# Attention over a long context: the division by the softmax sums goes from TensorE and VectorE to GpSimd by way of DRAM, and side work is dealt out evenly

## The chip, the cores and the metric

The kernel runs on one core of a Trainium2 chip. The metric is device time in microseconds of one launch. The core has five instruction streams: TensorE (PE, matrix products, with its weight loads shown as PEld), VectorE (DVE), ScalarE (ACT), GpSimd (POOL) and SyncE (SP), which here issues nearly all DMAs. Each stream runs its instructions in order and waits for the others by semaphores. SBUF is the on-chip memory with 128 partitions; PSUM is where PE writes and where DVE and ACT read its results.

## The reference

Four layers of cross-attention are applied to x (2048 tokens of 256) over one context of 1601 rows of 512. Layers L0, L2 and L3 are of one kind, "masked": 16 heads of 64.

```python
q = hidden_states @ Wq;  k = encoder_hidden_states @ Wk;  v = encoder_hidden_states @ Wv
logits = jnp.einsum('bhqd,bhkd->bhqk', q, k) * scale
logits = logits + col_bias[None, None, :, :]
probs = jax.nn.softmax(logits, axis=-1)
out = jnp.einsum('bhqk,bhkd->bhqd', probs, v)
out = out @ Wo + bo + residual
```

`col_bias` is zero but in up to four columns of the context, which the token indices name; there it is -20 for suppressed query rows. Layer L1 is "grouped": x is normalised by its root mean square, there are 16 query heads of 16 that share 4 key and value heads, and no bias. Everything is float32.

## The kernel before

**Tiles and units.** The tokens are four blocks b of 512 queries (QB), the context 13 chunks of 128 keys (NT = 13, the last has 65). Heads are taken in pairs: a "block" of a masked layer is one pair with its own slices of Wq, Wk, Wv and Wo (8 blocks a layer), a block of L1 has two pairs ("subs"; 4 blocks). A "unit" is one pair and one b. There are 128 units: 32 of each layer, 96 of them masked.

**Steps.** One loop of `N + NT + DELAY + LAG` steps, with N = 128*13, deals out the work, a chunk c a step. In a step the unit ka makes scores for its chunk ca; the unit kb, 15 steps behind, subtracts the row maxima and takes exponentials of its chunk cb; the unit kv, one step more behind, multiplies chunk cv with the values. In steps ca = 0 and 1 the maxima of the unit just scored are found and spread (L805, L806, L818). PE, DVE and ACT keep this written order: the last lines of the kernel add it as a dependency. POOL and SP get their order from the framework's scheduler.

**A masked step.** PE makes scores of both heads into a tile of `ps_s` (L751; two buffers, one tile is 128x1024). ACT copies it to a tile `p` of SBUF (L763; 17 buffers), DVE keeps a running maximum `top` (L768), and later adds the negated maxima (L834). ACT takes the exponential in place (L841). POOL adds the chunk to `sums` (L844 for chunks 0 and 1 together, L846 after that). PE multiplies with the values into `po` (L869). The trace has two matmul records for each float32 matmul of 512 columns.

**The tail of a unit.** After its last chunk ACT copies `po` to `oT` (L875, one buffer, 128 rows = 2 heads of 64, 512 queries). Four more pieces follow: `denominators` transposes `sums` with eight PE transposes into a tile of `ps_s` (L888), DVE reduces it (L889) and takes reciprocals (L890) into `rden`, 128x8, and POOL copies them 64 times side by side into `by` (L899). `divide` transposes `by` with four PE transposes (L907) and multiplies with `oT` on DVE (L911). `project(k)`, k = 0 and 1, is one matmul with Wo (L917), which DVE adds to the residual `xs` (L923). In L1 the sums are an extra row of the values' product; they come by four small matmuls (L894) and a reciprocal (L897).

**Pieces.** What isn't a chunk of a unit is a "piece", popped between the chunks at the end of a step: the tail of the unit before, the next unit's queries (L420, two pieces), and the next block's keys (L369, in groups of four pieces, one for the 65 keys) and values (L384, in groups of two). A group that has begun is finished before another queue is looked at. `urgent` (tail, queries) goes before `fill` (keys, values). Each step earns credit, and each piece costs one. No piece is popped in the two steps of a masked unit's maxima. Nearly every piece writes a tile of `ps_m` ("pm"), which has one buffer.

```python
def step(self, share):
    self.credit = min(self.credit + share, 2.0)
    while self.credit >= 1.0:
        self.pop()
        self.credit -= 1.0
...
pieces.step(max(1.0, (pieces.left() + 6 * after_this) / steps))
```

**Loads.** The transposed context lies in DRAM (`ctxT`); slices of it (`ct`, three buffers) come in by SP just ahead of the pieces that use them (L204), as do x (L735), the weights (L345, two buffers each) and Wo (L353).

Of the kernel before, what the change touches and what calls it, by code (L numbers as in the profile page):

```python
# [10 lines left out]
FP = mybir.dt.float32  # L11
# [18 lines left out]
def tile_cross_attention_stack(ctx: ExitStack, tc: tile.TileContext, t: dict, out: bass.AP):  # L30
# [167 lines left out]
    def context_slice(a, n):  # L198

        step = NCT if n <= 256 else NCT // 2  # L200
        tiles = []
        for k in range(0, NCT, step):
            ct = work.tile([P, step, 2 * QB // step], FP, name="ct", bufs=3)
            nc.sync.dma_start(out=ct[:, :, :n], in_=ctxT_dram[:, k : k + step, a : a + n])  # L204
            tiles.append(ct)
        return lambda k, b, m: tiles[k // step][:, k % step, b - a : b - a + m]
# [121 lines left out]
    class Masked:  # L328
# [8 lines left out]
        def load(self, n):  # L337
# [4 lines left out]
            u.wk = weights.tile([P, NCT, P], FP, name="wk")  # L342
            u.wv = weights.tile([P, NCT, P], FP, name="wv")
# [85 lines left out]
    class Grouped:  # L429
# [34 lines left out]
        def load(self, n):  # L464
# [3 lines left out]
            if n == 0:  # L468
# [14 lines left out]
                self.wk = weights.tile([P, NCT, 2, 64], FP, name="wk")  # L483
                self.wv = weights.tile([P, NCT, 64], FP, name="wv")
# [180 lines left out]
    def keep(l, b):  # L665
        nc.sync.dma_start(out=xT_dram[l][b], in_=xs[:, b])

    def normalize(l, b):
# [3 lines left out]
        def squares():  # L672
            held["x"] = work.tile([P, NC, QB], FP, name="xT")
            nc.scalar.activation(held["x"], xs[:, b], AF.Square)

# [10 lines left out]
        def divide(q):  # L686
# [8 lines left out]
            if q == QT - 1:  # L695
                nc.sync.dma_start(out=xT_dram[l][b], in_=held["x"])

        return [[squares], [rms], *([lambda q=q: divide(q)] for q in range(QT))]

    def rows_out(b):  # L700
# [9 lines left out]
        for q0 in (0, half):  # L710
# [5 lines left out]
            )  # L716


    class Unit:
# [116 lines left out]
        def exp(self, c, spare):  # L836
            u = self.u
            a, m = TCH[c]
            if self.masked:
                p = self.p[c]  # L840
                nc.scalar.activation(p[:m], p[:m], AF.Exp)  # L841
                if c == 1:
                    self.sums = work.tile([P, 2, QB], FP, name="sums")
                    nc.gpsimd.tensor_tensor(self.sums, self.p[0], p, ALU.add)  # L844
                elif c:
# [35 lines left out]
        def denominators(self):  # L881

            rden = self.rden = small.tile([P, 2, QT], FP, name="rden")
            if self.masked:
                pt = ps_s.tile([P, 2, QT, P], FP, name="s")
                for h in range(2):
                    for q in range(QT):
                        nc.tensor.transpose(pt[:, h, q, :], self.sums[:, h, ts(q, P)], ident)  # L888
                nc.vector.tensor_reduce(rden, pt, AX.X, ALU.add)  # L889
                nc.vector.reciprocal(rden, rden)  # L890
            else:
# [6 lines left out]
            self.by = work.tile([P, QT, 2, 64], FP, name="by", bufs=1)  # L898
            nc.gpsimd.tensor_copy(  # L899
                self.by,  # L900
                rden.rearrange("p h (q o) -> p q h o", o=1).to_broadcast((P, QT, 2, 64)),
            )

        def divide(self):
            pr = ps_m.tile([P, QB], FP, name="pm")
            for q in range(QT):
# [258 lines left out]
```

## Time and profile before

| | |
|---|---|
| median of 3 runs | 5645.32 us (5644.31 to 5645.62) |
| the profiled execution | 5653.54 us, its span 5651.8 us |
| PE busy | 5321.4 us, 94% |
| DVE, ACT, POOL busy | 71%, 57%, 50% |
| mean granted TensorE clock | 0.98 |
| DMA | 252.88 MB, mean 45 GB/s |

A group's line gives source line, engine, operation, output and inputs with partitions x elements and type, the count, busy time in us and mean ns of one instruction; behind the last bar stands the idle time of the engine just before these instructions and what ended it. Busy time of a group counts overlapping records once. A line of the waits gives who waited for whom, the total in us, how often and the longest. In the order of time a line begins with start and duration; a remark in brackets is the idle time of that engine just before, and who ended it.

### The profile page before, as it was taken

The numbers are of one execution on the slowest core, as the hardware profiler recorded it, in microseconds if no ns is written. First come the engines' busy times: TensorE is split into PE (matmuls) and PEld (weight loads), VectorE is DVE, ScalarE is ACT, GpSimd is POOL, SyncE is SP. The second block draws the span as 40 slices with busy tenths as digits, with TensorE's granted clock in tenths as the row PEclk, the third lists the DMA queues.
The fourth block names the chain that finished last, engine by engine and source line by source line (L and its number), as shares of the span: only waits on it lengthen the run. The fifth ranks groups of instructions, "written<-read, shape, count | busy, mean of one in ns | idle before, by whom it ended". The sixth has DMA issues, their size and how long they took to land.

```text
span 5651.8 us, 59516 instructions
## 1 busy us (share of the span) xinstructions
PE 5321.4 (94%) x22444; PEld 1865.2 (33%) x22444; DVE 4013.6 (71%) x4140; ACT 3196.2 (57%) x3513; POOL 2837.7 (50%) x1380
## 2 busy tenths in 40 slices
PE   6999999998889999999999999999999999999997
PEld 3333333332323333233233333333333333333332
DVE  3777777777765555555567777777777777777786
ACT  2666666665433434333456666666666666666665
POOL 1766666665410000000056666666666666666676
PEclk8999999999889999999999999999999999999998
DMA  4112211111100000001012111212111121111100
GB/s 135 32 57 60 59 49 53 55 56 44 39 20 5 9 9 9 9 13 52 15 51 61 56 54 49 57 56 59 46 56 55 54 59 49 53 56 52 54 17 15
DMA packets 209744, 252.88 MB, mean 45 GB/s; under 512 B 43529, under 2 KB 155401, under 8 KB 209456
## 3 DMA queue, kind: packets, MB, share of 16 engines
q1 hardware_dynamic: 206192, 243.69, 14.8%
q8 instruction: 177, 2.90, 0.2%
q0 software_dynamic: 1152, 3.28, 0.2%
q10 hardware_dynamic: 2112, 2.10, 0.1%
q14 instruction: 111, 0.91, 0.1%
HBM read 235.27 MB, written 13.76 MB: 44 GB/s over the span
## 4 chain that ended last, share of the span: by engine, by line
PE 78%; ACT 7%; POOL 7%; DVE 5%; issue 2%; DMA 0%; SPq 0%; ACTq 0%; POOLq 0%; DVEq 0%
PE po L869 24%; PE s L751 20%; PE pm L384 6%; PE pm L369 5%; PE pm L917 5%; POOL sums L844 4%; ACT p L763 4%; ACT p L841 3%; POOL sums L846 3%; PE s L850 2%; PE s L784 2%; PE pm L420 2%; PE s L805 2%; PE b L818 2%; PE s L855 2%
## 5 line engine op out<-in xcount | busy, mean ns | idle before, releaser
L846 POOL TENSOR_TENSOR sums<-sums,p 128x1024 f32<-128x1024 f32 (+1 forms) x1056 | 2499.2, 2367 | 1097.9 <-ACT p L841 1084.8
L763 ACT COPY p<-s 128x1024 f32<-128x1024 f32 (+1 forms) x1248 | 1263.4, 1012 | 1434.0 <-PE s L751 1138.3
L869 PE MATMUL po<-p,v 128*64 128x512 f32 (+1 forms) x6656 | 1821.7, 626 | 36.5 <-ACT p L841 34.7
L768 DVE TENSOR_TENSOR top<-s,top 128x1024 f32<-128x1024 f32 (+1 forms) x1056 | 1291.5, 1223 | 753.9 <-ACT p L763 749.4
L751 PE MATMUL s<-q,kT 64*128 64x512 f32 (+1 forms) x4992 | 1426.3, 648 | 117.6 <-DVE top L768 116.4
L834 DVE TENSOR_TENSOR p<-p,b 128x1024 f32<-128x1024 f32 (+1 forms) x1248 | 1504.7, 1206 | 2.4 <-PE b L818 2.0
L841 ACT ACTIVATE p<-p 128x1024 f32<-128x1024 f32 (+1 forms) x1248 | 1321.5, 1059 | 110.3 <-DVE p L834 109.4
L869 PEld LDWEIGHTS po<-p,v 128*64 128x64 f32 (+1 forms) x6656 | 332.0, 136 | 1032.1 <-issue 698.9
L899 POOL COPY by<-rden 128x512 f32<-128x512 f32 x128 | 78.5, 613 | 1111.8 <-DVE rden L897 1083.9
L751 PEld LDWEIGHTS s<-q,kT 64*128 64x128 f32 (+1 forms) x4992 | 370.7, 182 | 732.7 <-issue 454.6
L859 ACT ACTIVATE p<-s 128x1024 f32<-128x1024 f32 (+1 forms) x283 | 289.8, 1024 | 451.0 <-PE s L855 450.9
L844 POOL TENSOR_TENSOR sums<-p 128x1024 f32<-128x1024 f32 x96 | 226.5, 2360 | 434.2 <-ACT p L841 434.2
L789 DVE TENSOR_REDUCE row_top<-s 128x2 f32<-128x1024 f32 x261 | 318.6, 1221 | 122.9 <-PE s L784 121.9
L384 PEld LDWEIGHTS pm<-wv,ct 128*128 128x128 f32 (+1 forms) x2392 | 284.7, 187 | 218.9 <-issue 215.9
L384 PE MATMUL pm<-wv,ct 128*128 128x128 f32 (+1 forms) x2392 | 337.6, 286 | 0.5 <-ACT v L389 0.5
L369 PE MATMUL pm<-ct,wk 128*128 128x512 f32 (+1 forms) x736 | 315.8, 544 | 2.7 <-ACT kT L374 2.7
L917 PE MATMUL pm<-o,wo 128*128 128x512 f32 x512 | 292.0, 653 | 7.1 <-DVE xs L923 2.9
L859 ACT ACTIVATE p<-b 128x1024 f32<-128x1024 f32 (+1 forms) x133 | 136.2, 1024 | 217.8 <-PE b L855 217.8
L923 DVE TENSOR_TENSOR xs<-pm,xs 128x512 f32<-128x512 f32 x232 | 158.4, 683 | 90.4 <-PE pm L917 90.4
L806 DVE TENSOR_REDUCE ntop<-s 128x8 f32<-128x1024 f32 x96 | 117.6, 1225 | 130.9 <-PE s L805 130.6
L789 DVE TENSOR_REDUCE row_top<-b 128x2 f32<-128x1024 f32 x123 | 150.2, 1221 | 62.2 <-PE b L784 61.6
L420 PE MATMUL pm<-xT,wq 128*128 128x512 f32 x336 | 188.5, 644 | 0.0
(191 smaller groups left out, 3279.2 us busy)
## 6 DMA issues: line engine op xcount, KB each, us to landing
ct<-ctxT SPq DMA_DIRECT2D x288, 512.0 KB, 3.8
xT<-xT SPq DMA_DIRECT2D x104, 512.0 KB, 3.5
ct<-ctxT SPq DMA_DIRECT2D x48, 130.0 KB, 2.6
wk<-in_L_xattn_Wk_dram SPq DMA_DIRECT2D x24, 256.0 KB, 4.4
wv<-in_L_xattn_Wv_dram SPq DMA_DIRECT2D x24, 256.0 KB, 3.1
xT<-xs SPq DMA_DIRECT2D x12, 512.0 KB, 2.6
wq<-in_L_xattn_Wq_dram SPq DMA_DIRECT2D x24, 128.0 KB, 2.1
wo<-in_L_xattn_Wo_dram SPq DMA_DIRECT2D x24, 128.0 KB, 2.1
```

Source lines behind the costliest of these rows:

```text
L369: nc.tensor.matmul(u.pk[:, :n], u.wk[:, k, :], ct(k, a, n), start=(k == 0), stop=(k == NCT - 1),)
L384: nc.tensor.matmul(u.pv[:m, c - c0, :], ct(k, a, m), u.wv[:, k, :], start=(k == 0), stop=(k == NCT - 1),)
L751: nc.tensor.matmul(s[:m, h, :], self.u.kT[r, a : a + m], self.q[r, :], start=True, stop=(a != TAIL),)
L763: nc.scalar.copy(p[:m], s[:m])
L768: nc.vector.tensor_tensor(self.top[:m], s[:m], self.top[:m], ALU.max)
L789: nc.vector.tensor_reduce(self.top[:, :, q, k : k + 1], s, AX.X, ALU.max)
L834: nc.vector.tensor_tensor(self.p[c][:m], self.p[c][:m], self.less[:m], ALU.add)
L841: nc.scalar.activation(p[:m], p[:m], AF.Exp)
L844: nc.gpsimd.tensor_tensor(self.sums, self.p[0], p, ALU.add)
L846: nc.gpsimd.tensor_tensor(self.sums[:m], self.sums[:m], p[:m], ALU.add)
L869: nc.tensor.matmul(self.po[r, :], u.v[:m, c, r], self.p[c][:m, h, :], start=(c == 0), stop=(c == NT - 1),)
L917: nc.tensor.matmul(py, wo[:, ts(k, P)], self.o, start=True, stop=True)
```

## The change

The first chunk of `sums` is copied by POOL at c = 0, and every later chunk is added; before, the first addition took chunks 0 and 1 together. The denominators come a head at a time, four transposes each, into `ps_m` in place of `ps_s`, and cost half a credit each. `rden` is written to DRAM by SP (`cols`) and read back twice with a step of zero across 64 partitions, so that `by` holds a head's 512 reciprocals on each of that head's 64 rows. `divide` is one multiplication on POOL, in place in `oT`, for no credit; the four transposes of `by`, POOL's copy and DVE's multiplication are gone. `project` reads `oT`.

The tail is no longer put on the queue at once: queries are due one step after they were, the denominators three steps after the unit's last chunk, `divide` and `project` eight steps after it. A step earns what is left divided by the steps left, no longer at least one, and a piece tells its cost. Context tiles are loaded as their forerunners are used up, three ahead. `wk` and `wv` have one buffer each. The loop runs ten steps longer.

```diff
@@ -197,13 +197,16 @@
         step = NCT if n <= 256 else NCT // 2
-        tiles = []
-        for k in range(0, NCT, step):
-            ct = work.tile([P, step, 2 * QB // step], FP, name="ct", bufs=3)
+        tiles = {}
+        def load(k):
+            tiles[k] = ct = work.tile([P, step, 2 * QB // step], FP, name="ct", bufs=3)
             nc.sync.dma_start(out=ct[:, :, :n], in_=ctxT_dram[:, k : k + step, a : a + n])
-            tiles.append(ct)
-        return lambda k, b, m: tiles[k // step][:, k % step, b - a : b - a + m]
+        loads = [lambda k=k: load(k) for k in range(0, NCT, step)]
+        return lambda k, b, m: tiles[k - k % step][:, k % step, b - a : b - a + m], loads
...
@@ -339,8 +342,8 @@
             u.wq = weights.tile([P, NC, P], FP, name="wq")
-            u.wk = weights.tile([P, NCT, P], FP, name="wk")
-            u.wv = weights.tile([P, NCT, P], FP, name="wv")
+            u.wk = weights.tile([P, NCT, P], FP, name="wk", bufs=1)
+            u.wv = weights.tile([P, NCT, P], FP, name="wv", bufs=1)
             for to, w in ((u.wq, "Wq"), (u.wk, "Wk"), (u.wv, "Wv")):
...
@@ -480,8 +483,8 @@
                         nc.gpsimd.tensor_copy(self.last_k[:, g, to], ident[:, j : j + 16])
-                self.wk = weights.tile([P, NCT, 2, 64], FP, name="wk")
-                self.wv = weights.tile([P, NCT, 64], FP, name="wv")
+                self.wk = weights.tile([P, NCT, 2, 64], FP, name="wk", bufs=1)
+                self.wv = weights.tile([P, NCT, 64], FP, name="wv", bufs=1)
                 for half in range(2):
...
@@ -714,6 +720,16 @@
+    def on_all_partitions(cols, to):
+        rows = dram.tile([2, P, QT], FP, name="cols", bufs=4)
+        with nc.allow_non_contiguous_dma(reason="1024 values, four at a time"):
+            nc.sync.dma_start(out=rows.rearrange("h p q -> p h q"), in_=cols)
+        for tile_, heads_ in to:
+            src = rows[heads_].rearrange("(o h) p q -> o (h p q)", o=1)
+            nc.sync.dma_start(out=tile_, in_=src.to_broadcast(tile_.shape))
...
@@ -839,10 +855,10 @@
                 nc.scalar.activation(p[:m], p[:m], AF.Exp)
-                if c == 1:
+                if c == 0:
                     self.sums = work.tile([P, 2, QB], FP, name="sums")
-                    nc.gpsimd.tensor_tensor(self.sums, self.p[0], p, ALU.add)
-                elif c:
+                    nc.gpsimd.tensor_copy(self.sums, p)
+                else:
                     nc.gpsimd.tensor_tensor(self.sums[:m], self.sums[:m], p[:m], ALU.add)
...
@@ -878,15 +894,18 @@
-        def denominators(self):
-            rden = self.rden = small.tile([P, 2, QT], FP, name="rden")
+        def denominators(self, h):
+            if h == 0:
+                self.rden = small.tile([P, 2, QT], FP, name="rden")
+            rden = self.rden
             if self.masked:
-                pt = ps_s.tile([P, 2, QT, P], FP, name="s")
-                for h in range(2):
-                    for q in range(QT):
-                        nc.tensor.transpose(pt[:, h, q, :], self.sums[:, h, ts(q, P)], ident)
-                nc.vector.tensor_reduce(rden, pt, AX.X, ALU.add)
+                pt = ps_m.tile([P, QT, P], FP, name="pm")
+                for q in range(QT):
+                    nc.tensor.transpose(pt[:, q, :], self.sums[:, h, ts(q, P)], ident)
+                nc.vector.tensor_reduce(rden[:, h, :], pt, AX.X, ALU.add)
+                if h == 0:
+                    return 0.5
                 nc.vector.reciprocal(rden, rden)
...
@@ -895,26 +914,27 @@
                 nc.vector.reciprocal(rden, pd.rearrange("p q h -> p h q"))
-            self.by = work.tile([P, QT, 2, 64], FP, name="by", bufs=1)
-            nc.gpsimd.tensor_copy(
-                self.by,
-                rden.rearrange("p h (q o) -> p q h o", o=1).to_broadcast((P, QT, 2, 64)),
+            by = work.tile([P, P, QT], FP, name="by", bufs=1)
+            on_all_partitions(
+                rden,
+                [(by[self.rows(h)].rearrange("r p q -> r (p q)"), slice(h, h + 1)) for h in range(2)],
             )
+            self.by = by.rearrange("r p q -> r q p")
+            return 0.5 if self.masked else 1.0
+        def denominator_groups(self):
+            return [[lambda h=h: self.denominators(h)] for h in range(2 if self.masked else 1)]
         def divide(self):
-            pr = ps_m.tile([P, QB], FP, name="pm")
-            for q in range(QT):
-                nc.tensor.transpose(
-                    pr[:, ts(q, P)], self.by[:, q].rearrange("p h o -> p (h o)"), ident
-                )
-            self.o = work.tile([P, QB], FP, name="o", bufs=1)
-            nc.vector.tensor_tensor(self.o, pr, self.oT, ALU.mult)
+            oT = self.oT.rearrange("r (q p) -> r q p", p=P)
+            nc.gpsimd.tensor_tensor(oT, oT, self.by, ALU.mult)
+            return 0.0
             wo = self.layer.wo(self.u, self.sub)
-            nc.tensor.matmul(py, wo[:, ts(k, P)], self.o, start=True, stop=True)
+            nc.tensor.matmul(py, wo[:, ts(k, P)], self.oT, start=True, stop=True)
             to = xs[:, self.b, k, :]
...
@@ -923,9 +943,7 @@
         def finish_groups(self):
-            return [[self.denominators], [self.divide]] + [
-                [lambda k=k: self.project(k)] for k in range(NC)
-            ]
+            return [[self.divide]] + [[lambda k=k: self.project(k)] for k in range(NC)]
...
@@ -976,19 +994,20 @@
                 if not queue:
-                    return
+                    return 1.0
                 self.now.extend(queue.popleft())
-            self.now.popleft()()
+            cost = self.now.popleft()()
+            return 1.0 if cost is None else cost
-            self.credit = min(self.credit + share, 2.0)
+            self.credit = min(self.credit, 0.9) + share
             while self.credit >= 1.0:
-                self.pop()
-                self.credit -= 1.0
+                self.credit -= self.pop()
...
@@ -1010,33 +1029,30 @@
         nxt = made[l, n] = layer.load(n)
-        slices = {}
-        ahead = deque()
-        def load(name):
-            if name in ahead:
-                ahead.remove(name)
-                kind, c, a, width = name
-                slices[kind, c] = context_slice(a, width)
+        slices, loads = {}, deque()
                 if name:
-                    ahead.append(name)
-                def head(name=name, piece=group[0]):
-                    load(name)
-                    if name and ahead:
-                        load(ahead[0])
-                    piece()
-                found.append([head, *group[1:]])
+                    kind, c, a, width = name
+                    slices[kind, c], tiles = context_slice(a, width)
+                    loads.extend(tiles)
+                    each = len(group) // len(tiles)
+                    def read(j, piece, each=each):
+                        piece()
+                        if (j + 1) % each == 0 and loads:
+                            loads.popleft()()
+                    group = [lambda j=j, piece=piece, r=read: r(j, piece) for j, piece in enumerate(group)]
+                found.append(list(group))
             return found
         first, second = map(with_loads, layer.key_groups(nxt, slices))
+        for _ in range(min(3, len(loads))):
+            loads.popleft()()
...
@@ -1062,9 +1078,10 @@
     N = len(units) * NT
+    due = {}
     turn = 0
-    for step in range(N + NT + DELAY + LAG):
+    for step in range(N + NT + DELAY + LAG + 10):
         ka, ca = divmod(step, NT)
...
@@ -1077,6 +1094,7 @@
                 start_block(i)
+        top = of[ka - 1] if 0 < ka <= len(units) and ca < 2 else None
         three = not (scoring and scoring.masked) and not (exping and exping.masked)
...
@@ -1086,7 +1104,6 @@
-        top = of[ka - 1] if ka and ca < 2 and ka - 1 < len(units) else None
         if step == 3:
...
@@ -1104,10 +1121,11 @@
             ahead = unit_of(ka + 1)
-            pieces.urgent.extend(ahead.layer.unit_groups(ahead))
+            due.setdefault(step + 1, []).extend(ahead.layer.unit_groups(ahead))
         if valuing and cv == NT - 1:
-            pieces.urgent.extend(valuing.finish_groups())
-            pieces.urgent.extend(after(kv))
+            due.setdefault(step + 3, []).extend(valuing.denominator_groups())
+            due.setdefault(step + 8, []).extend(valuing.finish_groups() + after(kv))
+        pieces.urgent.extend(due.pop(step, ()))
...
@@ -1116,7 +1134,7 @@
             steps = NT - ca + (NT - 2) * after_this
-            pieces.step(max(1.0, (pieces.left() + 6 * after_this) / steps))
+            pieces.step((pieces.left() + 5 * after_this) / steps)
         elif not scoring:
     pieces.flush(pieces.urgent)
```

Three functions that issue no matmul (`keep`, `squares`, the normalising `divide`) now return a cost of 0.0; these lines are left out.

More of the change, by code (lines that the diff above doesn't have):

```diff
@@ L674, in squares @@
             nc.scalar.activation(held["x"], xs[:, b], AF.Square)
+            return 0.0
         def rms():
@@ L696, in divide @@
                 nc.sync.dma_start(out=xT_dram[l][b], in_=held["x"])
+            return 0.0
         return [[squares], [rms], *([lambda q=q: divide(q)] for q in range(QT))]
@@ L897, in denominators @@
                 nc.vector.reciprocal(rden, pd.rearrange("p q h -> p h q"))
-            self.by = work.tile([P, QT, 2, 64], FP, name="by", bufs=1)
-            nc.gpsimd.tensor_copy(
-                self.by,
-                rden.rearrange("p h (q o) -> p q h o", o=1).to_broadcast((P, QT, 2, 64)),
-            )
+            by = work.tile([P, P, QT], FP, name="by", bufs=1)
+            on_all_partitions(
+                rden,
+                [(by[self.rows(h)].rearrange("r p q -> r (p q)"), slice(h, h + 1)) for h in range(2)],
+            )
+            self.by = by.rearrange("r p q -> r q p")
+            return 0.5 if self.masked else 1.0
+        def denominator_groups(self):
+            return [[lambda h=h: self.denominators(h)] for h in range(2 if self.masked else 1)]
         def divide(self):
-            pr = ps_m.tile([P, QB], FP, name="pm")
-            for q in range(QT):
-                nc.tensor.transpose(
-                    pr[:, ts(q, P)], self.by[:, q].rearrange("p h o -> p (h o)"), ident
-                )
-            self.o = work.tile([P, QB], FP, name="o", bufs=1)
-            nc.vector.tensor_tensor(self.o, pr, self.oT, ALU.mult)
+            oT = self.oT.rearrange("r (q p) -> r q p", p=P)
+            nc.gpsimd.tensor_tensor(oT, oT, self.by, ALU.mult)
+            return 0.0
         def project(self, k):
```

## The prediction

> **What bounds the kernel now.** Four views, in this order: busy time by engine, TensorE's waits, the groups of instructions by shape, and the order of time around one wait.
>
> ```profile
> span 5651.8 us, 59516 instructions
> PE 5321.4 (94%) x22444; PEld 1865.2 (33%) x22444; DVE 4013.6 (71%) x4140; ACT 3196.2 (57%) x3513; POOL 2837.7 (50%) x1380
> ```
> ```profile
> PE s L751 <- DVE top L768: 116.4, 71, 2.7
> PE pm L907 <- POOL by L899: 55.9, 79, 4.4
> ```
>
> PE is busy 94% of the span: every PE microsecond taken away or added moves the end. Its two largest waits belong to the tail of a unit, which the change rewrites.
>
> ```profile
> L917 PE MATMUL pm<-o,wo 128*128 128x512 f32 x512 | 292.0, 653 | 7.1 <-DVE xs L923 2.9 <-DVE xs L921 2.3 <-DVE o L911 1.9
> L907 PE MATMUL pm<-ident,by 128*128 128x128 f32 x512 | 90.5, 303 | 56.1 <-POOL by L899 55.9
> L846 POOL TENSOR_TENSOR sums<-sums,p 128x1024 f32<-128x1024 f32 x960 | 2271.8, 2366 | 1025.6 <-ACT p L841 1015.1 <-ACT ka L517 3.5 <-ACT v L389 2.4
> L899 POOL COPY by<-rden 128x512 f32<-128x512 f32 x128 | 78.5, 613 | 1111.8 <-DVE rden L897 1083.9 <-DVE rden L890 26.8
> L791 DVE TENSOR_REDUCE row_top<-b 128x8 f32<-128x520 f32 x11 | 7.7, 701 | 10.0 <-PE b L784 9.9
> ```
>
> An ordinary masked step, in order of time (start, duration):
>
> ```profile
> 3402.84 1.13 PE L751 MATMUL s<-q,kT 64*128 64x512 f32 x4
> 3404.91 1.12 PE L369 MATMUL pm<-ct,wk 128*128 128x512 f32 x2
> 3404.98 1.06 ACT L841 ACTIVATE p<-p 128x1024 f32<-128x1024 f32 x1
> 3405.11 1.22 DVE L768 TENSOR_TENSOR top<-s,top 128x1024 f32<-128x1024 f32 x1 [0.77 <-ACT p L763]
> 3405.96 1.13 PE L751 MATMUL s<-q,kT 64*128 64x512 f32 x4
> 3406.18 2.37 POOL L846 TENSOR_TENSOR sums<-sums,p 128x1024 f32<-128x1024 f32 x1 [0.76 <-ACT p L841]
> ```
>
> The step is 3.12 us. PE comes to its piece 2.07 us after the step's start; DVE finishes `top` at 3.49; POOL starts the step's sum at 3.34 and ends it at 5.71. These offsets carry the sum below. Now a tail whose two parts fall into one step:
>
> ```profile
> 4342.24 1.09 PE L888 MATMUL s<-ident,sums 128*128 128x128 f32 x8
> 4342.71 1.01 ACT L763 COPY p<-s 128x1024 f32<-128x1024 f32 x1 [1.84 <-POOL sums L844]
> 4344.90 1.21 DVE L889 TENSOR_REDUCE rden<-s 128x8 f32<-128x1024 f32 x1
> 4347.11 0.61 POOL L899 COPY by<-rden 128x512 f32<-128x512 f32 x1
> 4347.77 0.66 PE L907 MATMUL pm<-ident,by 128*128 128x128 f32 x4 [4.44 <-POOL by L899]
> 4348.36 1.97 PE L751 MATMUL s<-q,kT 64*128 64x512 f32 x4
> ```
> ```profile
> 4348.00:4352.00 4.00, 4.00 (x12) 0.88 (x10) 2.35 (x3) 1.58 (x2) 0.00 (x0) 0.57 0.00 0
> ```
>
> A wait of 4.44 us for a product of POOL, and after it the granted clock is 0.57 of full over 4 us (the column after the five engines): the scores take 1.97 us instead of 1.13, the values 1.89 instead of 1.08. The clock costs 1.7 us on top. After the like wait at 2890.8 us the four groups of matmuls that follow lose 2.8 us, at 0.50 for 6.5 us.
>
> **What goes.** (a) 512 transposes of `by`: 90.5 us of PE. (b) The waits before them: 56. (c) The masked denominators no longer take a tile of `ps_s`, so the next scores needn't wait for `top`: 112 of the 116.4 us (68 waits of 1.65 directly behind L888). The copy at c=0 frees p[0] a step earlier, which ends ACT's 1.84 us; PE feels that only through (c), so it is counted once. Sum 259. The copy itself (two 512s at 613 ns, 1.2 us a unit), the multiply and twelve sums make 31 us of POOL in a unit of some 43: covered by the steps' POOL idle (0.76 us and more before each sum). DVE loses L911 and has slack. The even sharing leaves 112 masked steps without a piece instead of 32; such a step takes 2.07 us of PE at 3 isolated places of the trace, so PE's work only changes place: nothing, or up to 15 us if DVE (2.43 us a step) falls behind.
>
> **What comes, counted in the built program of the changed kernel.**
>
> (1) A wait on `pm`, which has one buffer. Head 1's four transposes, or another piece, follow head 0's or head 1's denominators within one step 86 times (63 times head 1 behind head 0). The first four end 2.07+0.55 = 2.62 us into the step; the reduction comes behind `top` (3.49) and takes 0.70 (row of 520); PE goes on at 4.25. Each 1.65 us; two L917 in one step waited up to 1.4 in this trace with 0.55 us more work ahead, which makes it 1.3 to 1.95. Sum 142.
>
> (2) The projection waits for the multiply. The denominators are due five steps before `divide`, but a key group of four pieces is not interrupted, so they slip. Of four units of a block the last denominators come 3, 2, 1 and 1 steps before the projection. `divide` costs no credit, so `project(0)` follows in the same step; and on POOL the multiply stands behind the sum of that very step in 45 masked units. In these PE arrives at 2.07, the sum ends at 5.71, and a multiply of 1.2 us (half of L846) ends at 6.9, with its handover 7.0. Units whose previous step held the two heads' wait have DVE 0.9 us late against PE, which its `subtract` hands on: 5.5; the others 4.9. I take 5.2: 234 us. The chain that feeds it, reciprocal 0.2, a write to DRAM, two broadcasts and their issues, is bounded by DMA rows:
>
> ```profile
> wq<-in_L_xattn_Wq_dram SPq DMA_DIRECT2D x24, 128.0 KB, 2.1
> wo<-in_L_xattn_wo_dram SPq DMA_DIRECT2D x16, 16.0 KB, 1.7
> ```
>
> Write 1.7 to 2.1, reads 2.1 plus one issue of 0.35: about 4.5 us, so `by` lands some 10.3 us after the start of the denominators' step, and the sum (10.5 to 11 on that scale) is still last. In 19 units with two steps between, the multiply follows the previous step's sum and ends 0.4 us late: 10 with a few odd ones. With three steps it is hidden behind them. On SP a context load stands between write and broadcasts in 19 units and waits for PE's key piece; it is issued at about 5.4, its 512 KB take 3.8, and the broadcasts behind it still land before that sum ends. So xT and context loads, which are two tiles (some 12 us) ahead, stay hidden too; their cover ends if SP blocks longer than that. `wk`, `wv` with one buffer are loaded before their first use by half a block or more: nothing.
>
> (3) The clock. 45 waits above 4.44 us, each with 1.7 to 2.8 behind it as measured: 2.3, so 104 us. Nothing is the lower bound, since most of the 1.65 us waits had no drop; but three of three above 4.4 us had one.
>
> (4) Layer L1 (32 units). POOL is free there; the chain is reciprocal 0.57 after the products, DRAM and back 4.6, multiply 1.2 and handovers: 6.6 us. A step without a piece is 2.1 us. The projection comes in the same step in 6 units (6.6), one step later in 13 (4.5), two in 9 (2.4): 40+58+22 = 120; clock for the first 19: 44. Before, L1's tail had no wait.
>
> (5) The end: DRAM and back in place of two short steps: 5.
>
> Sum 142+234+10+104+120+44+5 = 659, less 259: +400. The profiled execution took 5653.54 (span 5651.8), 8 above the median of 5645.3; so 5645+400 = 6045.
>
> **Two rules of the Trainium skill against this.** *GPSIMD Engine Reference*, Performance pitfalls, says that POOL reading SBUF in steps above 8 bytes pays about half again; `by` is read in steps of 16 bytes, and no run here shows it. By that the multiply is an estimated 1.8 us and 73 waits (45+28) grow by 0.6, +44. *TensorE: Matmul & The Clock Gate*, Part 1, says that an idle window of 3.4 us halves the clock until a busy one; the row above agrees (0.57). By one such window, 1.7 us a wait, (3) and (4) would be 109 instead of 148.
>
> **Rivals.**
> *Faster: PE's arrival is late enough that the multiply is never waited for.* Place: `project(0)`. If the product stands ready, what remains is -259+142, 5530. It decides below 117 us of such waits in all, 1.6 us on each of 73. For it: half of the masked units have two or three steps of cover. Against: 45 multiplies stand behind a sum that ends 3.6 us after PE's arrival.
> *Waits, but the clock holds:* +400-148, 5895. For: 68 waits of 1.65 us passed mostly undisturbed. Against: three waits of 4.44 us, three drops.
> *SP becomes the bound:* broadcasts held behind loads that wait for PE, 3 us more on the 73 waits, +220, 6265. For: 19 units have a load between. Against: SP's loads land in 2 to 4 us.
> *The spread makes no difference* (within 0.2%): the two sums would have to cancel.
>
> **How the numbers follow.** Forecast 0.72, clock holds 0.12, SP 0.08, faster 0.06, same 0.02. 0.2% (11 us) is about what a measurement of this kernel can tell from no change. Low end of the forecast: (1) at 1.3 us is 112, (2) at 4.9 is 220, the clock at 1.0 behind the 45 is 45, L1 with a chain of 5.8 is 6x5.8+13x3.7+9x1.6 = 97, the end and the rest 10: 484-259 = +225, 5870. High end: 86x1.95 = 168; 45x6.5 = 292 (the broadcasts 1 us late behind a context load); 30 for the 19 units; the clock 64x3.3 = 211 (half of 6.5 us); L1 with 7.5, 45+70+30 = 145; 25 for steps without pieces and the end: 871-259 = +612, 6257. I give 5880 to 6250; it takes in the clock rival. Faster 0.06, same 0.02, slower 0.92.
>
> **What would show it.** Right: PE waits on POOL before the projection, 4.9 to 5.5 us some 45 times and 2 to 7 us some 28 times in L1; about 86 waits of 1.65 on DVE between denominators; no L907; a granted clock below 0.95 in masked slices. Wrong: a wait for POOL below 120 us in total, a multiply that starts ahead of the step's sum, or DMAs back in under 2 us together.

## The result, and the profile after

The changed kernel takes 6248.9 us (median of 4 runs, 6246.4 to 6255.0), the kernel before took 5644.8 beside it: a ratio of 1.107 [1.105, 1.109], 604 us slower (by the ratio 606 on the 5645.3 from which the forecast starts), where the forecast was +400 and its range ended at +605. The direction and the place of the waits were as forecast; the size was a third short, and what ends the wait was another thing.

The first two lines of the page of the changed kernel:

```profile
span 6245.3 us, 59379 instructions
PE 5444.7 (87%) x21832; PEld 1840.7 (29%) x21932; DVE 3951.9 (63%) x4108; ACT 3191.9 (51%) x3513; POOL 3052.6 (49%) x1476
```

The span grew by 593.5 us. TensorE's busy time grew by 123.3, although 90.5 us of transposes are gone, so what is left took some 214 us longer, about 190 of it by the clock (the part on the prediction takes it apart). The rest, 470 us, is idle time of TensorE: 330 before, 801 after. No other engine came near to being full; POOL, which got the new work, is busy for 49%.

TensorE's waits in the changed kernel (who waits for whom, us in total, how often, the longest):

```profile
PE pm L937 <- POOL oT L930: 498.7, 108, 9.7
PE pm L905 <- DVE rden L906: 94.3, 65, 1.5
PE pm L372 <- DVE rden L906: 31.0, 19, 1.6
```

The first line is the projection waiting for POOL's product; 108 of 128 units have it. The second and third are pieces that wait until DVE has emptied the one buffer of `pm` behind a head's denominators. The two lines that led this view before are gone: `top` is down from 116.4 to 2.7 us, the transposes of `by` no longer exist. The groups of instructions by shape tell what stood behind the product itself:

```profile
L937 PE MATMUL pm<-oT,wo 128*128 128x512 f32 x512 | 381.2, 835 | 517.5 <-POOL oT L930 498.7 <-DVE xs L943 13.7 <-DVE xs L941 3.5
...
L930 POOL TENSOR_TENSOR oT<-oT,by 128x512 f32<-128x512 f32 x128 | 195.1, 1524 | 1454.3 <-DMA by<-cols 1439.2 <-ACT v L392 5.6 <-PE pm L387 3.9
```

The multiply takes 1.52 us. POOL's idle time before it is ended by the DMA `by`, not by its own sum: the reciprocals come back from DRAM last. In all 45 masked units whose projection comes in the denominators' step or in the next one, the second broadcast lands after POOL's last work before the multiply has ended. And the projection's matmuls take 835 ns each where the same group took 653: they run right behind a wait, on a lowered clock. The issues of DMAs (KB each, median us from issue to landing) give the trip:

```profile
by<-cols SPq DMA_DIRECT2D x256, 128.0 KB, 3.1
...
cols<-rden SPq DMA_DIRECT2D x128, 4.0 KB, 2.2
```

SP issues the first broadcast 0.06 us after the write has landed (median of 128 units), the second some 0.5 us later. So from the issue of the write to the landing of both broadcasts it is 6.0 us (median). One masked unit in order of time, whose last denominators come one step before its projection:

```profile
3757.72 0.66 PE L905 MATMUL pm<-ident,sums 128*128 128x128 f32 x4
...
3759.80 0.66 PE L905 MATMUL pm<-ident,sums 128*128 128x128 f32 x4 [1.43 <-DVE rden L906]
...
3761.22 0.20 DVE L909 RECIPROCAL rden<-rden 128x8 f32<-128x8 f32 x1
...
3761.45 0.36 SPq L729 DMA_DIRECT2D cols<-rden  x1
...
3763.74 2.34 POOL L862 TENSOR_TENSOR sums<-sums,p 128x1024 f32<-128x1024 f32 x1 [2.41 <-ACT p L857]
3764.72 1.12 SPq L732 DMA_DIRECT2D by<-cols  x2
3768.46 1.52 POOL L930 TENSOR_TENSOR oT<-oT,by 128x512 f32<-128x512 f32 x1 [2.38 <-DMA by<-cols]
3770.03 2.08 PE L937 MATMUL pm<-oT,wo 128*128 128x512 f32 x2 [7.50 <-POOL oT L930]
3772.04 2.08 PE L767 MATMUL s<-q,kT 64*128 64x512 f32 x4
```

Read it from the first line down. The two heads' denominators fall into one step, and the second waits 1.43 us for the buffer. The write leaves 0.23 us after the reciprocal has begun. POOL's sum of the projection's step ends at 3766.08; the broadcasts are there only at 3768.46, 7.0 us behind the write's issue. TensorE stood for 7.50 us, and the next scores take 2.08 us in place of 1.13. The same stretch in windows (length, then busy time of PE, PEld, DVE, ACT and POOL with counts, the granted clock, the DMA share and GB/s):

```profile
3750.00:3758.00 8.00, 7.95 (x29) 2.07 (x28) 6.53 (x7) 6.17 (x8) 6.87 (x3) 1.00 0.35 102
...
3766.00:3770.00 4.00, 0.00 (x0) 0.00 (x0) 0.00 (x0) 0.00 (x0) 1.60 (x2) 0.50 0.24 66
3770.00:3776.00 6.00, 5.97 (x11) 1.55 (x12) 2.56 (x3) 1.79 (x2) 0.00 (x0) 0.54 0.00 0
```

For 4 us, of the five engines POOL alone is busy, and for 1.60 us of them; for the 6 us after it TensorE is fully busy at 0.54 of its clock. Over the whole trace the clock stands at 0.50 for 820 us in 113 stretches; before it was 234 us in 35.

### The profile page after: what moved, and what is told of

Read it like the earlier page. It is cut to its first block, busy times and chain, and to the rows that moved or that the text cites. A ratio compares the mean times of both kernels' runs of the same rounds, so it can differ in the third digit from the quotient of the medians.

```text
span 6245.3 us, 59379 instructions
## 1 busy us (share of the span) xinstructions
PE 5444.7 (87%) x21832; PEld 1840.7 (29%) x21932; DVE 3951.9 (63%) x4108; ACT 3191.9 (51%) x3513; POOL 3052.6 (49%) x1476
## 4 chain that ended last, share of the span: by engine, by line
PE 71%; DMA 8%; DVE 8%; ACT 5%; POOL 4%; issue 3%; SPq 1%; POOLq 0%; ACTq 0%; DVEq 0%
PE po L885 20%; PE s L767 18%; PE pm L937 6%; PE pm L372 5%; DMA by<-cols 5%; PE pm L387 4%; PE pm L423 3%; DMA cols<-rden 3%; ACT p L779 3%; POOL oT L930 3%; DVE top L784 2%; PE s L866 2%; PE s L800 2%; PE b L834 2%; PE s L821 2%
## 5 line engine op out<-in xcount | busy, mean ns | idle before, releaser
L862 POOL TENSOR_TENSOR sums<-sums,p 128x1024 f32<-128x1024 f32 (+1 forms) x1152 | 2723.9, 2365 | 1482.8 <-ACT p L857 1459.7
L885 PE MATMUL po<-p,v 128*64 128x512 f32 (+1 forms) x6656 | 1846.0, 634 | 37.8 <-ACT p L857 25.9
L767 PE MATMUL s<-q,kT 64*128 64x512 f32 (+1 forms) x4992 | 1477.0, 669 | 4.4 <-DVE top L784 2.7
L930 POOL TENSOR_TENSOR oT<-oT,by 128x512 f32<-128x512 f32 x128 | 195.1, 1524 | 1454.3 <-DMA by<-cols 1439.2
L937 PE MATMUL pm<-oT,wo 128*128 128x512 f32 x512 | 381.2, 835 | 517.5 <-POOL oT L930 498.7
L937 PEld LDWEIGHTS pm<-oT,wo 128*128 128x128 f32 x512 | 95.6, 234 | 750.4 <-POOL oT L930 591.1
L905 PE MATMUL pm<-ident,sums 128*128 128x128 f32 x768 | 126.8, 288 | 96.9 <-DVE rden L906 94.3
```

Source lines behind the costliest of these rows:

```text
L767: nc.tensor.matmul(s[:m, h, :], self.u.kT[r, a : a + m], self.q[r, :], start=True, stop=(a != TAIL),)
L862: nc.gpsimd.tensor_tensor(self.sums[:m], self.sums[:m], p[:m], ALU.add)
L885: nc.tensor.matmul(self.po[r, :], u.v[:m, c, r], self.p[c][:m, h, :], start=(c == 0), stop=(c == NT - 1),)
L937: nc.tensor.matmul(py, wo[:, ts(k, P)], self.oT, start=True, stop=True)
```

## The experiments

The theory (A): TensorE takes its work in written order, and a latency of about 9 us (trip, multiply, handovers) was put into a place where one step of 3 us lies between; the even sharing lets the denominators slip towards the projection, and the lowered clock follows the waits. The rivals: the copy, the multiply's place on POOL or its 16-byte step, or SP's queue carry the loss; or the sharing alone does. The kernel before was timed again beside each of three groups of runs: 5650.6, 5646.5 and 5644.6 us (medians). Each ratio is against the time beside it.

| kernel | us | ratio [95%] | wait for the product | clock at half, us |
|---|---|---|---|---|
| before | 5644.8 | 1 | 1.9 (DVE's) | 234 |
| changed | 6248.9 | 1.107 [1.105, 1.109] | 498.7 | 820 |
| finish two steps later | 5944.8 | 1.053 [1.051, 1.054] | 164.5 | 428 |
| denominators first | 5608.9 | 0.993 [0.991, 0.994] | 17.5 | 157 |
| spread on the chip | 5854.0 | 1.036 [1.034, 1.038] | 107.9 (DVE's) | 207 |
| before, copy alone | 5540.2 | 0.981 [0.979, 0.983] | 1.9 (DVE's) | 155 |
| changed, old sharing | 5874.6 | 1.040 [1.038, 1.042] | 217.4 | 404 |
| first, heads apart | 5638.4 | 0.998 [0.998, 0.999] | 89.2 | 293 |
| multiply on DVE | 6407.2 | 1.135 [1.133, 1.137] | 564.1 | 932 |
| `by` without a step | 7370.7 | 1.306 [1.304, 1.308] | 1517.8 | 1896 |
| first, apart, +9 | 5551.3 | 0.983 [0.981, 0.984] | 18.4 | 156 |
| the same, no copy | 5631.8 | 0.998 [0.997, 0.999] | 18.8 | 136 |
| the same, old sharing | 5496.9 | 0.974 [0.972, 0.975] | 11.4 | 135 |
| before, even sharing alone | 5671.8 | 1.005 [1.003, 1.006] | 4.8 (DVE's) | 203 |

### The finish two steps later

```diff
-            due.setdefault(step + 8, []).extend(valuing.finish_groups() + after(kv))
+            due.setdefault(step + 10, []).extend(valuing.finish_groups() + after(kv))
```

> divide and project are due ten steps after the unit's last chunk instead of eight; nothing else changes. Theory A (the loss is PE's wait for the product, set by how few steps lie between the denominators and the projection, and the clock that drops behind each wait): in the masked layers 90 of 96 units now have three steps or more, so their waits (321 us of the 499) fall under 15; L1 gains little, 13 of its units still have at most one step (about 100 us left). The clock goes up to about 0.97. Time about 6249 - 380 - 130 = 5740. Theory B (the trip through DRAM and SP holds up SP's loads, and the even sharing leaves PE short in steps, wherever the projection stands): the time stays above 6100.

5944.8: two thirds of the waits for the product went, and half of the loss, 304 us; the forecast for this run was too good. TensorE's waits show what came instead:

```profile
PE pm L937 <- POOL oT L930: 164.5, 34, 9.1
PE pm L937 <- DVE xs L943: 103.5, 116, 3.3
...
PE pm L387 <- DVE rden L906: 31.8, 20, 1.7
```

So late, both projections of a unit fall into one step (in 125 units, in 17 before this edit), the second waiting for `pm` (103.5 us, 13.7 before this edit). The 34 waits left are mostly L1's. A later finish is half a remedy: it moves the consumer, while the producer is still late.

### The denominators ahead of everything

```diff
-            due.setdefault(step + 3, []).extend(valuing.denominator_groups())
+            due.setdefault(step + 1, [])[:0] = valuing.denominator_groups()
```

> the denominators are due one step after the unit's last chunk and ahead of the next unit's queries, so that four steps or more lie before the projection in nearly all units of all layers (L1 five or more). Theory A: waits for the product below 25 us, clock back to about 0.975, the 128 us of waits on pm between the two heads stay (49 units still have both heads in one step, about 75 to 130 us); 6249 - 475 - 190 = 5585, faster than before. Theory B: above 6100. A third theory, that the clock fell by itself with the denser schedule: waits gone but the clock still 0.94, about 5770.

5608.9, below the kernel before. One line of order takes 640 us from the changed kernel, with the DRAM trip, POOL's multiply, the copy and the sharing all in place. TensorE's waits, and its busy time on the page:

```profile
PE pm L905 <- DVE rden L906: 68.6, 51, 3.9
PE pm L423 <- DVE rden L906: 55.8, 37, 1.6
...
PE pm L937 <- POOL oT L930: 17.5, 3, 8.6
```
```profile
PE 5243.9 (93%) x21932; PEld 1795.9 (32%) x21932; DVE 3945.7 (70%) x4108; ACT 3190.0 (57%) x3513; POOL 3053.7 (54%) x1476
```

The wait for the product is 17.5 us in 3 places, and TensorE's busy time is down by 201 us with the same matmuls. The clock came back with the waits (157 us at half instead of 820), which shows that those 201 us were theirs.

### The spread back on the chip

```diff
-            by = work.tile([P, P, QT], FP, name="by", bufs=1)
-            on_all_partitions(
...
+            self.by = work.tile([P, QT, 2, 64], FP, name="by", bufs=1)
+            nc.gpsimd.tensor_copy(
+                self.by,
+                rden.rearrange("p h (q o) -> p q h o", o=1).to_broadcast((P, QT, 2, 64)),
             )
...
-            nc.gpsimd.tensor_tensor(oT, oT, self.by, ALU.mult)
-            return 0.0
+            pr = ps_m.tile([P, QB], FP, name="pm")
+            for q in range(QT):
+                nc.tensor.transpose(
+                    pr[:, ts(q, P)], self.by[:, q].rearrange("p h o -> p (h o)"), ident
+                )
+            nc.vector.tensor_tensor(self.oT, pr, self.oT, ALU.mult)
```

> the changed kernel with only the spread and the product put back: POOL copies rden 64 times, PE transposes, DVE multiplies; denominators a head at a time, copy of the first chunk, due steps and even sharing stay. Theory A: product waits fall to under 60 us and the clock comes back to 0.97; PE gets 90 us of transposes again, the pm waits of 128 us stay: 6249 - 440 - 190 + 90 = 5710, about 1% slower than before. Theory B with the even sharing as the cause: above 6000.

5854.0: without the DRAM trip the changed kernel is 395 us faster, but 203 slower than before, more than expected. TensorE's waits:

```profile
PE pm L939 <- DVE oT L933: 107.9, 83, 3.7
PE pm L905 <- DVE rden L906: 91.3, 65, 1.5
PE pm L939 <- DVE xs L945: 38.6, 48, 1.2
```

The changed order of the pieces puts two or three of the tail's pieces into a step (both heads 64 times, `divide` with a projection 82 times), and each follower waits for `pm` or for DVE. The clock is hardly touched (207 us at half, 234 in the kernel before); these waits are near 1.3 us. So the trip is one part of the loss; the crowding of the tail's pieces is another.

### The copy of the first chunk alone

```diff
-                if c == 1:
+                if c == 0:
                     self.sums = work.tile([P, 2, QB], FP, name="sums")
-                    nc.gpsimd.tensor_tensor(self.sums, self.p[0], p, ALU.add)
-                elif c:
+                    nc.gpsimd.tensor_copy(self.sums, p)
+                else:
```

> the kernel before with nothing but the copy of the first chunk. If ACT's 1.84 us wait for POOL's first sum is what made top late behind the denominators, the next scores wait some 0.4 us instead of 1.65 in 68 units: 5645 - 85 = 5560. If the tile of ps_s is what counts and not the late top, nothing: 5645 within 10.

5540.2, 1.9% (110 us) faster than before. ACT's and TensorE's waits in this kernel:

```profile
ACT p L763 <- POOL sums L844: 58.8, 86, 1.0
```
```profile
PE s L751 <- DVE top L768: 29.3, 71, 1.6
```

ACT's wait for the buffer p[0] falls from 174.5 to 58.8 us, TensorE's wait for `top` from 116.4 to 29.3. The copy is the good part of the change and clears itself of the loss.

### The old sharing in the changed kernel

```diff
-            self.credit = min(self.credit, 0.9) + share
+            self.credit = min(self.credit + share, 2.0)
...
-            pieces.step((pieces.left() + 5 * after_this) / steps)
+            pieces.step(max(1.0, (pieces.left() + 6 * after_this) / steps))
```

> the changed kernel with the credit of before (at least one a step, up to 2.0 kept); all else stays, the due steps too. In the built program 18 masked units instead of 45 have the multiply behind the sum of the projection's own step, 20 instead of 24 behind the one before, and in L1 no unit projects in the denominators' step and one (not 13) in the next. Theory A: the even sharing is itself half of the cause, because it starves the urgent pieces: waits 18 at 6.0, 20 at 2.1, L1 one at 5.9 and 12 at 3.0 = 190 us instead of 499, the clock gives back some 110: 6249 - 310 - 110 = 5830. Theory B (the trip through DRAM as such, however the pieces are shared): within 60 us of 6249.

5874.6. With at least one credit a step the denominators are popped earlier, and over half of the loss goes, without a change to the trip:

```profile
PE pm L937 <- POOL oT L930: 217.4, 79, 9.2
PE pm L387 <- DVE rden L906: 63.7, 39, 1.6
```

The product's wait falls by 281 us and the busy time by 102; together that is within 9 of the 374 us gained; other waits changed little in sum. What the sharing spreads, it takes from pieces that are in a hurry.

### The heads apart, and then the finish a step later

```diff
                 if h == 0:
-                    return 0.5
+                    return 1.0
...
-            return 0.5 if self.masked else 1.0
+            return 1.0
```

This goes on top of the denominators first; the second run has in addition `step + 9` for the finish.

> denominators ahead of the queries as in the second experiment, and each head costs a whole credit, so that the heads come in different steps (4 units instead of 49 have both in one). If the rest of the loss is PE waiting for the one buffer of pm between two pieces of one step, the 124 us of such waits behind the denominators go to under 20: 5609 - 105 = 5505, faster than the copy alone (5540). If it is the even sharing or the load order, 5609 within 15.

> as the sixth experiment (denominators ahead of the queries, a step for each head), with divide and project due nine steps after the last chunk instead of eight. There 31 units had POOL's multiply behind the sum of the step before the projection and PE waited 2.2 us in each. Now every masked unit has two steps or more between that sum and the projection. Theory A: product waits under 25 us (the end of the kernel has some 18), the clock back to 0.985: 5638 - 72 - 65 = 5500, faster than the copy alone. Rival (the trip through DRAM has a price of its own on SP or on PE's matmuls): above 5600.

The first missed: 5638.4, 30 us worse than with half credits. The waits of 1.4 us behind a head's denominators went, as meant, but the second head came a step later, and some 31 units had the multiply behind the sum of the step before the projection, 2.2 us each:

```profile
PE pm L937 <- POOL oT L930: 89.2, 34, 9.0
PE pm L937 <- DVE xs L943: 49.3, 56, 1.7
```

One step more for the finish, and the first line is almost gone; 5551.3:

```profile
PE pm L937 <- DVE xs L943: 54.4, 63, 1.7
...
PE pm L937 <- POOL oT L930: 18.4, 3, 8.8
```

The two kernels differ by one number, the step in which the finish is due. By their traces TensorE's busy time fell by 52 us, which is the clock's share, and its idle time by 41: 71 of the product's wait, less what other waits gave back. A chain that is late by 2 us in a third of the masked units cost 87 us of time.

### The multiply on DVE

```diff
-            nc.gpsimd.tensor_tensor(oT, oT, self.by, ALU.mult)
+            nc.vector.tensor_tensor(oT, oT, self.by, ALU.mult)
```

> the changed kernel with the product of oT and by on DVE instead of POOL; everything else as changed. Prediction as recorded (POOL's sum of the same step ends last): each of the 45 waits loses the rest of that sum and the longer multiply, 1.5 us or more. Theory A2 (the broadcasts land last, POOL waits 1 us for them after its sum): each of some 95 waits loses only the difference of the multiplies, 1.52 on POOL against some 0.65 on DVE, 0.87 us: 83 us and some 25 of clock, 6140. If DVE's standing still at its wait costs its own work, above 6200.

6407.2: worse by 158 us than on POOL. The multiply itself is shorter (1.07 us), and in units whose denominators came one step ahead the wait fell from 6.0 to 5.2 us. But DVE keeps the written order, so the multiply stands behind the `top` of its step, and DVE with all that follows stands until the broadcasts land (263.2 us of DVE's idle time end with them). Units with three steps or more, which waited 0.35 us, now wait 4.5:

```profile
PE pm L937 <- DVE oT L930: 564.1, 122, 9.0
```

That the multiply sits behind POOL's sum was therefore not the cause, as the broadcasts that land after the sum had said; that on POOL it isn't held to the written order was a help.

### `by` without the 16-byte step

```diff
-        rows = dram.tile([2, P, QT], FP, name="cols", bufs=4)
+        rows = dram.tile([2, QT, P], FP, name="cols", bufs=4)
...
-            nc.sync.dma_start(out=rows.rearrange("h p q -> p h q"), in_=cols)
+            nc.sync.dma_start(out=rows.rearrange("h q p -> p h q"), in_=cols)
...
-            by = work.tile([P, P, QT], FP, name="by", bufs=1)
+            by = work.tile([P, QT, P], FP, name="by", bufs=1)
```

> by and its rows in DRAM are laid out block after block, so that POOL reads by in steps of 4 bytes instead of 16, and the write to DRAM has 1024 pieces of 4 bytes instead of 256 of 16. If the step of 16 bytes is what makes the multiply 1.52 us instead of half of the sum's 2.37, it becomes 1.18; 95 waits shorten by 0.34, 32 us, and time is some 6210, unless the write of 4-byte pieces takes more than 0.3 us longer. If not, the multiply stays 1.52 and the time 6249.

A miss of 1160 us, and the clearest run on the cause. To have the reciprocals lie flat, the write has to scatter 1024 pieces of 4 bytes in place of 256 of 16, and that price had not been counted. The DMA issues, and the group of the multiply:

```profile
cols<-rden SPq DMA_DIRECT2D x128, 4.0 KB, 10.6
```
```profile
L930 POOL TENSOR_TENSOR oT<-oT,by 128x512 f32<-128x512 f32 x128 | 161.5, 1261 | 2552.7 <-DMA by<-cols 2506.3 <-ACT p L779 46.4
```

The write lands after 10.6 us instead of 2.2, and the wait for the product rises to 1517.8 us: in units whose denominators come one step before the projection it is 14.2 us in place of 6.0, 8.2 more for a write that is 8.4 longer; with two steps it is 10.6 in place of 2.3. Once the cover is used up, the trip's length goes into the wait one for one, and the clock's price comes on top. The multiply, which was the question, takes 1.26 us flat and 1.52 with the step: a fifth more. The Trainium skill, *GPSIMD Engine Reference*, Performance pitfalls for Q7 kernels, states about half more for such steps; for this two-input multiply the runs show 21%.

### Which parts are worth keeping

Two runs take the best kernel so far (first, apart, +9) and undo one part of the change each, with the edits shown above for the copy and the sharing; the third puts the even sharing alone into the kernel before.

> the kernel of e9 with the sums as before (chunks 0 and 1 added at c=1, no copy). If the copy is worth what it was alone, some 110 us, because ACT's wait of 1.84 us reaches PE wherever the denominators stand: about 5610. If the wait reaches PE only through a late top behind the denominators, which now come later or in other steps: within 20 us of e9.

> the kernel of e9 with the credit of before (at least one a step). If the even sharing is worth something by itself once the projection never waits, e9 is faster than this by 20 us or more. If it only moves pieces, within 15 us. If the half-empty steps it makes cost PE, this one is faster.

> the kernel before with nothing but the even sharing of credit (what is left by the steps left, at most 0.9 kept). Theory A: it slows the tail's pieces but there is no DRAM trip behind them, so within 1% of before, 5600 to 5700; more pieces share a step with another and wait for pm, some 0.8 to 1.6 us each, so rather above. Rival (even sharing itself is the cause of the loss): above 5800.

Without the copy: 5631.8, 80 us slower. So the copy's worth isn't tied to `top`'s wait, which the separate `pm` tile has already ended here; TensorE's largest wait is another one:

```profile
PE po L885 <- ACT p L857: 105.5, 156, 7.5
```

It is 29.7 us with the copy: without it ACT waits 210.1 us for POOL to give p[0] back (53.9 with it), and is late with the exponentials.

With the old sharing: 5496.9, a ratio of 0.974 [0.972, 0.975] to the kernel before and the fastest of all. TensorE's waits and the page's line of busy time:

```profile
PE pm L937 <- DVE xs L943: 73.6, 78, 2.4
...
PE pm L937 <- POOL oT L930: 11.4, 2, 8.9
```
```profile
PE 5236.2 (95%) x21932; PEld 1798.6 (33%) x21932; DVE 3935.3 (72%) x4108; ACT 3202.0 (58%) x3513; POOL 3051.9 (55%) x1476
```

The busy time is 85 us below that of the kernel before. That lies within 6 us of the prediction's own subtraction (5321.4 - 90.5 = 5230.9), but partly by chance, since the clock and the split transposes of `sums` move it too. A fairer measure is the copy alone, which keeps the transposes of `by` and has the clock at half for about as long (155 us, here 135):

```profile
PE 5287.9 (96%) x22444; PEld 1856.7 (34%) x22444; DVE 4011.6 (72%) x4140; ACT 3194.6 (58%) x3513; POOL 2934.3 (53%) x1476
```

Against it 52 us of busy time are saved, and some 40 us of time (5540.2 and 5496.9; ratios 0.981 and 0.974). That is what the rest of the change brings over the copy, with its pieces in the right order and the old sharing; no run takes the transposes' part out by itself. The even sharing alone, in the kernel before, costs 27 us (16 to 35 by the interval) with TensorE's busy time unchanged at 5321.4; in the best kernel it costs 54. It does not carry the loss by itself, but through the denominators that it delays.

## Where the prediction held, and the step that failed

By the prediction's own terms, in us, against the trace of the changed kernel:

| term | forecast | measured | from |
|---|---|---|---|
| what goes | -259 | -260 | 90.5 + 55.9 + (116.4 - 2.7) |
| (1) waits for `pm` | 142 | 128 | 94.3 + 31.0 + 2.4 |
| (2) and (4), waits for the product | 364 | 499 | the wait's line |
| (3) and (4), the clock | 148 | 192 | 123.3 + 90.5 - 22.1 |
| the transposes of `sums` in two groups | not in the sum | 22 | 126.8 - 104.7 |
| (5) the end and all else | 5 | 13 | remainder to 593.5 |

**What goes** was right, (a) to (c). One clause was not: TensorE feels the copy "only through (c)". The copy alone brings 110 us before the change and 80 with (c) in place, there by way of the wait for exponentials. As the change has both, the sum didn't suffer.

**(1)** was right in mechanism and size: 65 waits of 1.45 us and 19 of 1.63.

**(2), the projection waits for the multiply,** was right in place and wrong in what the multiply waits for, and so short by 102 us for masked units, 34 for L1. The step that failed is "`by` lands some 10.3 us after the start of the denominators' step, and the sum is still last". It rests on a trip of 4.5 us, which came from rows of larger and other DMAs: a write "1.7 to 2.1" and a read of 2.1 like `wq`'s, of the same 128 KB. The write took 2.2, but the broadcasts 3.1 each, so the trip is 6.0. It then ends after POOL's sum and not before. In the 42 masked units whose denominators come one step before the projection, that sum ended 3.55 us after PE's arrival (median), as forecast (5.71 - 2.07 = 3.64), but POOL then stood idle for another 1.0 us, and the multiply took 1.52 instead of 1.2: the wait is 6.0 us on average, where 5.2 was forecast (46 units whose denominators come one step before the projection or in its step: 282 us against 234). The same excess turned 24 units that have them two steps before from 0.4 into 2.3 us (55 against 10), and units with three or more, called hidden, gave another 9.

**(4)**, L1: waits of 7.8, 5.9, 3.0 and 0.85 us with the denominators none, one, two and three steps before the projection, in 6, 13, 9 and 4 units, where 6.6, 4.5, 2.4 and none were forecast: again the trip, which is 5.8 us there (median), where 4.6 was taken.

**(3), the clock:** forecast were 64 stretches at 2.3 us. Of the 214 us by which TensorE's busy time says more, 22 aren't the clock. The sum left out that the eight transposes of `sums` now come as two groups of four, 0.66 us each in the rows above, where eight in a row took 1.09. In the kernel before and in the changed one:

```profile
L888 PE MATMUL s<-ident,sums 128*128 128x128 f32 x768 | 104.7, 280 | 12.8 <-POOL sums L846 12.8
```
```profile
L905 PE MATMUL pm<-ident,sums 128*128 128x128 f32 x768 | 126.8, 288 | 96.9 <-DVE rden L906 94.3
```

With the denominators first, where the clock is restored, this group still takes 127.3 us. That leaves 192 us for the clock. Half of TensorE's busy time at half clock says nearly the same: 551 us after and 178 before, half of the difference is 187. With 78 stretches more than before that is 2.4 to 2.5 us each. So the price of one was right and their number too low: waits that the forecast had at 0.4 or 2.4 us came out at 2.3 and 3.0, and such waits lower the clock too. In the changed kernel the clock is at half within 3 us of the end of 93 of the 101 waits of 2 us or more, of 26 of the 37 between 1.5 and 2 us, and of 6 of the 92 between 1 and 1.5 us. The Trainium skill, *TensorE: Matmul & The Clock Gate*, Part 1, gives at least one idle window of about 3.4 us before the clock is halved and at least one busy one before it is full again; by one busy window it would be an estimated 1.7 us a wait. The trace has more behind a wait, and shorter waits suffice: with the heads apart, 29 of 33 waits of 2.0 to 2.5 us have the clock at half behind them.

**The rivals.** SP as the bound had the number nearest to the result (6265), for the wrong reason: the first broadcast leaves 0.06 us after the write has landed (median), and over 0.2 us after it in only 5 of 128 units, at most 1.1, so SP's queue hardly holds it. The faster rival needed less than 117 us of waits; there were 499. The even sharing's steps without a piece were put at "nothing, or up to 15"; the sharing made alone costs 27 us, but no run shows how much of that those steps are.

What stays open: why the even sharing costs these 27 to 54 us where no product is waited for. The idle time of TensorE is 23 us longer in the one case and 35 in the other, spread over several waits of some 10 to 20 us in total each; no run took it apart. The new order of the context loads and the single buffers of `wk` and `wv` were never undone by themselves either; they are in the best kernel too, so they don't carry the loss.

## What to carry to other kernels

Before moving a hand-over from engines to DRAM, count the steps between its producer and the in-order consumer, and set the whole chain (here 6.0 us of trip, 1.5 of multiply, and what the multiplier has queued in front) against them; what isn't covered goes into the consumer's wait one for one, and the lowered clock took about another 2.4 us behind most stalls of 2 us or more. If it doesn't fit, put the producer ahead of less urgent work before anything else: here that one line was worth 640 us, while a later consumer gave half of that and the multiply on another engine made it worse. And undo a change part by part even when the whole has lost: it held a copy worth 80 to 110 us, and with its pieces in the right order and the old sharing it is 2.6% faster than the kernel before, where the copy alone brings 1.9%.

## What the runs showed of the hardware that had not been expected

- The same 4 KB written to DRAM takes 2.2 us in 256 pieces of 16 bytes and 10.6 us in 1024 pieces of 4: (10.6 - 2.2) / 768 = 10.9 ns for each further piece, an estimate from these two.
- Reading 2 KB of DRAM onto 64 partitions (128 KB in all) lands after 3.1 us, where a weight load of the same 128 KB (`wo`) takes 2.1.
- POOL's copy of 128x1024 takes 1.04 us where its addition of the same size takes 2.37; the copy at c = 0 is thus cheaper than the sum it replaces, and comes a step earlier.
